# Quarter-block products in four more LSTM steps, with a new place for sums of weights and a later load of two groups of x

## The chip, the cores and the metric

The kernel runs on one core of one Trainium2 chip. The metric is the device time of one execution in microseconds; the median of three runs before the change is 2421.2 (2419.95 to 2422.31). Lower is better. All arithmetic is fp32.

## The reference

Four layers of a graph network act on x of shape 128 x 64 x 256 (128 graphs, 64 nodes, 256 features), each as `x = x + layer(max(layernorm(x), 0))`. The change lies in the first layer, in its last LSTM. That layer mixes the nodes twice with the adjacency matrix and small weights, and then runs four LSTMs, p = 1 to 4, each over windows of p consecutive nodes; the last hidden state of a window replaces its last node:

```python
def step(carry, x_t):
    h, c = carry
    g = x_t @ Wih.T + h @ Whh.T + bias
    i, f, gg, o = jnp.split(g, 4, axis=-1)
    c = jax.nn.sigmoid(f) * c + jax.nn.sigmoid(i) * jnp.tanh(gg)
    h = jax.nn.sigmoid(o) * jnp.tanh(c)
    return ((h, c), None)
...
for p in range(1, MAX_SKIP + 1):
    nw = Tv // p
    wins = h[:, :nw * p, :].reshape(Bv * nw, p, Hd)
    last = _lstm_last(Wih[p - 1], Whh[p - 1], bih[p - 1], bhh[p - 1], wins)
    idx = jnp.arange(nw) * p + (p - 1)
    h = h.at[:, idx, :].set(last.reshape(Bv, nw, Hd))
return h
```

The second layer is masked attention over the 64 nodes, the third two linear layers with batch normalization, the fourth three graph convolutions.

## The kernel before

**Tiling.** The 8192 tokens lie in 16 groups of 512 (`NG`), a group being 4 tiles of 128 tokens. Four groups (`NK` = 4) have x tiles of their own from the start, `xs[0]` to `xs[3]`, under the tags x0 to x3. The state of the first layer lies transposed in four tiles `hs[0]` to `hs[3]`, 32 graphs each, with features on the partitions.

**The LSTMs.** The loop at L896 runs p = 1 to 4. A unit (L905) is a run of windows in two of the four `hs` tiles: 256 windows of each, for p = 4. There are four units at p = 4, taken in pairs: j = 0 is the pair on `hs[0]` and `hs[1]`, j = 2 the pair on `hs[2]` and `hs[3]`. A pair first takes its first time step (`first_steps`, L762), which has no hidden state yet, and then, for t = 1 to p - 1, each unit of the pair in turn takes `next_step` (L813). So j = 2 at p = 4 has six such steps, numbered by `slot` from 0 to 5: two units at t = 1, two at t = 2, two at t = 3.

**Seven products.** A step works out two gate sets (`gate_set`, L694: i with g, then f with o). The product of a gate set's weights with x and h is a 2 x 2 block product, done with seven block products instead of eight (`seven`, L241, with the sums and differences of Winograd's form of Strassen's method). Each block product is itself a product of 2 x 2 quarter blocks of 128 x 128 weights with 256 columns of data, four matmuls of 256 columns. The profile shows an fp32 matmul as two records. The sums of weights are made once per p (`blocks_of`, L865), the differences of data by DVE in each step (L821 to L827).

**Quarter blocks.** Where a step gets `within`, two of its seven block products per gate set, numbers 6 and 2, are split once more (`Split`, L178): seven matmuls of 128 columns instead of four of 256. This needs four sums of quarter weights per split product, made once per p by `split_sums` (L885), and eight differences of quarter data per step, made by DVE in `split_differences` (L225). Each split product comes out of TensorE in two parts: `first` (four products, L197), which ACT copies out once (L207), DVE adds up (L209, L210) and POOL adds to three quarters (L213); and `last` (three products), which DVE adds (L223). Steps without `within` add a whole bank with one DVE instruction (L262) and let ACT apply a gate's function straight from the bank.

**Room.** While the LSTMs run, the tags x0 to x3 hold four scratch tiles `free[0]` to `free[3]` (L895). `free[0]` and `free[1]` hold the sums of quarter weights, `free[2]` and `free[3]` the scratch of the pair's two units. Steps have `within` at p = 2 and at p = 4 with j = 0. At p = 4 with j = 2, x is loaded again into those tags (L928 to L932), so that `within` is None there. The weights of the LSTMs and their sums lie in a pool of five tiles (`lw`, tag w). At p = 4 two of them hold the weights and two the sums that all steps use; p = 3 had used the other tiles for its weights and half of its sums.

**Beside the last six steps.** During j = 2 DVE turns the finished nodes of `hs[0]` and `hs[1]` round (`turn_nodes`, L387, two parts in each of slots 0 to 3), and SP writes them to memory as y. In slots 2 and 3, `x_for` (L372) loads four groups of x each into the tiles that `hs[0]` and `hs[1]` leave. `add_turned` (L400) is a DMA that POOL issues and that adds y to a group of x. The tuple `ADDED_BESIDE` (L167) says which groups are added in which slot, behind POOL's last sum of the step: groups 0 and 1 in slot 2, 2 and 3 in slot 3, 4 and 5 in slot 4, 6 and 7 in slot 5. In slot 4 group 0 is normalized for the attention. Groups 1 and 2 are normalized by `normalized` (L1080): group 1 at the start of the attention's first group, group 2 at its end.

**Order.** Each engine's instructions are put in order before the run by a planner that simulates their times and takes ready instructions in the order of the program text; `tc.issue_after(x)` puts an instruction behind x on its engine. Instructions may thus stand earlier or later than in the text. In the profile, attention's first matmul (L1118) starts at 1197.27 us.

Of the kernel before, what the change touches and what calls it, by code (L numbers as in the profile page):

```python
# [9 lines left out]
F32 = mybir.dt.float32  # L10
# [5 lines left out]
P = 128  # L16
D = 256
# [8 lines left out]
NK = PER  # L26
# [13 lines left out]
def adj_preln_kernel(ctx: ExitStack, tc: tile.TileContext, x_in, adj, vec, bg0, bg1,  # L40
# [17 lines left out]
    def load_x(x, g):  # L58
        nc.sync.dma_start(out=x, in_=x_view[:, g * GT : (g + 1) * GT, :])
# [104 lines left out]
    HN = GN // 2  # L164

    sums_on_pool = []
    ADDED_BESIDE = ((), (), (0, 1), (2, 3), (4, 5), (6, 7))  # L167

    def summed_last():
        return sums_on_pool[-1]  # L170
# [256 lines left out]
    with tc.tile_pool(name="lw", bufs=5) as lw:  # L427
# [6 lines left out]
        with tc.tile_pool(name="gw", bufs=1) as gw, tc.tile_pool(name="gcn", bufs=2) as gp, \  # L434
# [84 lines left out]
            for i, w_d in enumerate((wg0, wg1)):  # L519
                w = gw.tile([P, 2, D], F32, tag=f"wg{i}", name=f"wg{i}")  # L520
# [149 lines left out]
        with tc.tile_pool(name="back", bufs=1, reuse_waits="tile") as back_pool, \  # L670
# [194 lines left out]
            def blocks_of(p, wi, wh):  # L865


                wx, wm = (w.rearrange("p c (j m f) -> p m c j f", m=2, f=P) for w in (wi, wh))
                ss = []
                for tag, pool in (("w", lw), ("w", lw) if p == 4 else ("arena", keep)):  # L870
                    s = pool.tile([P, 2, 1024], F32, tag=tag, name="s")
                    ss += [s[:, :, i * 512 : (i + 1) * 512] for i in range(2)]
                ss = [s.rearrange("p c (j f) -> p c j f", f=P) for s in ss]

                def make(which):
                    sums(nc.vector, wx[:, 0], wm[:, 0], wx[:, 1], wm[:, 1], *ss, which=which)

                make(range(3))
                within = None
                if p != 3:  # L880
                    within = {}
                    for i, a, s in ((6, ss[1], free[0]), (2, wm[:, 0], free[1])):
                        blocks = [[a[:, c, 2 * r : 2 * r + 2] for c in range(2)] for r in range(2)]
                        s = s.rearrange("p a (i f) -> p a i f", f=P)
                        split_sums(nc.vector, blocks, s)  # L885
                        within[i] = blocks, s
                ws = [by_chunk([wx[:, m], wm[:, m]]) for m in range(2)] + [by_chunk(ss)]
                return ws, lambda: make([3]), within
# [7 lines left out]
            for p, nk in ((1, 8), (2, 8), (3, 7), (4, 8)):  # L896
                n = nk * HB
                wi, wh = w_next
                if p < 4:
                    w_next = (load_w(wih, p), load_w(whh, p))  # L900
                starts = range(0, NODES // p // nk * nk, nk)
                units = [(tiles, k0) for tiles in ((0, 1), (2, 3)) for k0 in starts]

                for j in range(0, len(units), 2):
                    two = [unit(p, *u, nk) for u in units[j : j + 2]]  # L905
                    first_steps(p, n, two, units[j : j + 2], w0)
                    if p > 1:
                        flush()
                        if j == 0:
                            ws, last_sum, within = blocks_of(p, wi, wh)  # L910
                    if j + 2 == len(units):
                        if p < 4:
                            w0 = first_blocks(
                                w_next[0], weight_tile(),
                                [copied_of[i] for i in (9, 14, 15, 15)] if p == 1 else None,
                            )
                        else:
                            w_att = weight_tile()
                            nc.sync.dma_start(
                                out=w_att[:, :, 0:768], in_=wqkv.rearrange("(c p) f -> p c f", p=P)  # L920
                            )
                            wqk = [[w_att[:, c, m * D : (m + 1) * D] for c in range(2)] for m in range(2)]
                            wv = w_att[:, :, 512:768]
                            ss = [w_att[:, c, 768:1024] for c in range(2)]
                            nc.vector.tensor_tensor(ss[0], wqk[1][0], wqk[1][1], ALU.add)
                            nc.vector.tensor_tensor(ss[1], ss[0], wqk[0][0], ALU.subtract)
                            nc.vector.tensor_tensor(wdiff, wqk[0][0], wqk[1][0], ALU.subtract)
                    if p == 4 and j == 2:  # L928
                        within = None
                        for g in range(NK):  # L930
                            xs[g] = xpool.tile([P, GT, D], F32, tag=f"x{g}", name=f"x{g}")
                            load_x(xs[g], g)  # L932
                    for t in range(1, p):
                        for i, u in enumerate(two):
                            stepped_before = stepped
                            stepped = next_step(
                                t, p, n, u, ws, last_sum if (j, t, i) == (0, 1, 0) else None,
                                (within, free[2 + i]) if within else None,
                            )

                            if p == 4 and j == 2:
                                slot = 2 * t + i - 2
                                if slot == 0:
                                    room = keep.tile([P, 2, TN, 2, 32], F32, tag="arena", name="turned")
                                for part in range(2 * slot, min(2 * slot + 2, 8)):
                                    turn_nodes(
                                        part,
                                        room[:, part % 3] if part % 3 < 2 else back_pool.tile(
                                            [P, TN, 2, 32], F32, tag="hc", name="turned"
                                        ),  # L950
                                    )()
                                for x_of_group in ADDED_BESIDE[slot]:
                                    with tc.issue_after(summed_last()):
                                        add_turned(x_of_group)
                                if slot in (2, 3):
                                    x_for(slot - 2)
                            if p == 4 and j == 2 and t == p - 1 and i == 0:

                                h = back_pool.tile([P, GT, D], F32, tag="hc", name="h")
                                with tc.issue_after(stepped_before):  # L960
                                    ln_relu(xs[0], h)
                                hTs = keep.tile([P, 2, 2, GN], F32, tag="arena", name="hT")
                                hT = features(transposed(h))
# [540 lines left out]
    for g in range(NG):  # L1504
        a = h1s[g]
# [83 lines left out]
    room = w_att[:, :, 512:1024]  # L1589
# [303 lines left out]
    within = None  # L1893
# [112 lines left out]
```

## Time and profile before

| | before |
|---|---|
| median of three runs | 2421.2 us |
| profiled execution | 2423.3 us |
| its span (first to last instruction) | 2421.5 us |
| mean granted clock of TensorE | 0.999 |
| DVE, ACT, POOL busy | 70%, 49%, 25% |
| p = 4, j = 0: its six split steps | 890.6 to 1033.2 us |
| p = 4, j = 2: first time step | 1033.2 to 1051.4 us |
| p = 4, j = 2: six steps | 1051.4 to 1197.3 us |

The three engines DVE, ACT and POOL work on what TensorE left in its eight banks of PSUM, and on what it will read next. The span is what the profile accounts for; the rest of the execution lies around it. In the profile a PE record's length is modelled and reaches into the next record, so the pace of matmuls is read from start to start.

### The profile page before, as it was taken

What the parts mean: (1) busy time and instruction counts of PE and PEld (TensorE: products, weight loads), DVE (VectorE), ACT (ScalarE), POOL (GpSimd) and SP (SyncE); (2) the same over time, 40 slices, a digit from 0 to 9 for tenths busy, and PEclk for the clock granted to TensorE, in tenths of its full rate; (3) what the DMA queues carried; (4) which work ended last, traced back from release to release, by engine and by line L of the source; (5) the groups of instructions that cost most, each with busy time, mean ns of one, the idle gap of its engine ahead of it and who ended that gap; (6) DMA issues with size and microseconds to landing.
All of it is one profiled execution on the core that took longest, in us unless ns stands there. A gap on an engine that the chain in (4) does not pass through costs nothing.

```text
span 2421.5 us, 49124 instructions
## 1 busy us (share of the span) xinstructions
PE 2398.7 (99%) x20272; PEld 2094.3 (86%) x20272; DVE 1685.4 (70%) x3425; ACT 1177.2 (49%) x2178; POOL 605.9 (25%) x549
## 2 busy tenths in 40 slices
PE   9999999999999999999999999999999999999999
PEld 7778888889999999988888867586898999999998
DVE  6768888777566687775599887586556655665664
ACT  4557755555444454453455556564333334333332
POOL 4432222222111112212224444123111311221121
PEclk9999999999999999999999999999999999999999
DMA  4200000001000000053347410010133100000000
GB/s 139 86 2 1 1 18 1 1 1 35 1 1 1 1 1 1 18 127 70 53 78 133 76 32 2 10 62 10 27 62 57 33 10 11 19 10 10 19 10 19
DMA packets 163712, 75.45 MB, mean 31 GB/s; under 512 B 104481, under 2 KB 159905, under 8 KB 163489
## 3 DMA queue, kind: packets, MB, share of 16 engines
q1 hardware_dynamic: 150096, 59.18, 9.8%
q0 software_dynamic: 12672, 12.58, 3.5%
q8 instruction: 159, 2.61, 0.4%
q14 instruction: 65, 0.52, 0.1%
q10 hardware_dynamic: 720, 0.56, 0.1%
HBM read 42.94 MB, written 20.97 MB: 26 GB/s over the span
## 4 chain that ended last, share of the span: by engine, by line
PE 92%; DVE 5%; ACT 2%; issue 1%; POOL 0%; DVEq 0%; ACTq 0%; POOLq 0%
PE ps L704 37%; PE ps L1772 13%; PE ps L1824 8%; PE ps L197 7%; PE ps L1700 4%; PE ps L146 4%; PE ps L1096 3%; PE ps L612 2%; PE ps L638 2%; PE ps L1470 2%; PE ps L1022 2%; PE ps L1055 2%; PE ps L1532 1%; PE ps L1118 1%; PE ps L1845 1%
## 5 line engine op out<-in xcount | busy, mean ns | idle before, releaser
L718 ACT ACTIVATE gates<-gates,lbias 128x512 f32<-128x512 f32 (+3 forms) x482 | 265.7, 605 | 173.7 <-DVE gates L272 121.6
L704 PE MATMUL ps<-diff,s 128*128 128x256 f32 (+1 forms) x1600 | 344.9, 369 | 0.5 <-DVE diff L826 0.5
L704 PEld LDWEIGHTS ps<-diff,s 128*128 128x128 f32 x1600 | 303.3, 190 | 27.5 <-issue 0.9
L1772 PE MATMUL ps<-arena 128*128 128x256 f32 x1408 | 318.5, 380 | 0.0
L267 POOL TENSOR_TENSOR gates<-p 128x512 f32<-128x512 f32 (+1 forms) x115 | 148.9, 1295 | 589.0 <-DVE p L263 518.4
L1772 PEld LDWEIGHTS ps<-arena 128*128 128x128 f32 x1408 | 261.4, 190 | 35.1 <-issue 2.0
L704 PE MATMUL ps<-h,w 128*128 128x256 f32 (+1 forms) x1028 | 242.5, 371 | 0.0
L704 PE MATMUL ps<-diff,w 128*128 128x256 f32 (+1 forms) x1040 | 239.7, 371 | 0.0
L704 PEld LDWEIGHTS ps<-diff,w 128*128 128x128 f32 x1040 | 194.8, 190 | 16.5
L704 PEld LDWEIGHTS ps<-h,w 128*128 128x128 f32 x1028 | 192.7, 190 | 17.7 <-issue 0.5
L267 POOL TENSOR_TENSOR arena<-arena 128x512 f32<-128x512 f32 (+1 forms) x80 | 91.7, 1147 | 461.9 <-DVE arena L263 407.8
L256 ACT COPY p<-ps 128x512 f32<-128x512 f32 (+1 forms) x262 | 142.1, 563 | 60.1 <-PE ps L704 39.7
L350 ACT ACTIVATE arena<-arena 128x512 f32<-128x512 f32 x168 | 98.5, 624 | 121.4 <-POOL arena L267 66.5
L256 ACT COPY arena<-ps 128x512 f32<-128x512 f32 (+1 forms) x160 | 82.2, 517 | 149.6 <-PE ps L1700 59.5
L1824 PE MATMUL ps<-arena 128*128 128x128 f32 x1280 | 149.1, 275 | 0.8 <-DVE arena L339 0.8
L1824 PEld LDWEIGHTS ps<-arena 128*128 128x128 f32 x1280 | 146.7, 192 | 2.1 <-DVE arena L339 1.2
L718 ACT ACTIVATE gates<-ps,lbias 128x256 f32<-128x256 f32 (+2 forms) x157 | 68.2, 479 | 143.9 <-PE ps L704 143.8
L339 DVE TENSOR_TENSOR arena<-arena 128x512 f32<-128x512 f32 (+1 forms) x192 | 111.3, 612 | 29.4 <-ACT arena L350 27.8
L207 ACT COPY free<-ps 128x128 f32<-128x128 f32 x104 | 27.6, 265 | 208.0 <-PE ps L197 208.0
L272 DVE TENSOR_TENSOR gates<-p,ps 128x512 f32<-128x512 f32 (+1 forms) x115 | 76.3, 664 | 65.0 <-PE ps L704 64.2
L704 PE MATMUL ps<-state,s 128*128 128x256 f32 (+1 forms) x512 | 116.3, 370 | 0.6 <-ACT p L256 0.6
L272 DVE TENSOR_TENSOR arena<-arena,ps 128x512 f32<-128x512 f32 (+1 forms) x80 | 48.1, 601 | 87.0 <-PE ps L1824 50.4
(270 smaller groups left out, 4831.0 us busy)
## 6 DMA issues: line engine op xcount, KB each, us to landing
x<-in_x SPq DMA_DIRECT2D x23, 512.0 KB, 4.0
y<-turned SPq DMA_DIRECT2D x64, 128.0 KB, 3.3
v<-vt SPq DMA_DIRECT2D x128, 64.0 KB, 2.6
w<-in_wih SPq DMA_DIRECT2D x4, 1024.0 KB, 7.2
x_for_h<-in_x SPq DMA_DIRECT2D x8, 512.0 KB, 6.9
x<-y POOLq DMA_DIRECT2D x8, 512.0 KB, 6.3
x_for_h<-y POOLq DMA_DIRECT2D x8, 512.0 KB, 6.7
z<-w SPq DMA_DIRECT2D x64, 64.0 KB, 2.0
```

The costliest lines, as they stand in the source:

```text
L146: last = nc.tensor.matmul(pss[b][half * 64 : half * 64 + 64, c, t, :], lhsT=src[rows, t, col : col + 64], rhs=a2[rows, :], start=True, sto ...
L197: nc.tensor.matmul(q[k], lhsT=w, rhs=b, start=first and k == 0, stop=True, skip_group_check=True)
L256: copied = nc.scalar.copy(p1 if i == 1 else p5, ps[i])
L267: nc.gpsimd.tensor_tensor(out=out[1][1], in0=p1, in1=p5, op=ALU.add).ins
L272: nc.vector.tensor_tensor(out[0][1], p1, ps[5], ALU.add)
L339: last = eng.tensor_tensor(out=s, in0=p, in1=q, op=op)
L350: nc.scalar.activation(o, o, func)
L704: nc.tensor.matmul(ps[:, r], lhsT=wc[:, j, :], rhs=bc, start=first and r == 0 and c == 0, stop=True, skip_group_check=True,)
L718: nc.scalar.activation(o, ps, func, bias=lbias[:, col : col + 1])
L1700: nc.tensor.matmul(ps[:, t, :], lhsT=w[:, t * P : (t + 1) * P], rhs=b, start=first and t == 0, stop=True, skip_group_check=True,)
L1772: nc.tensor.matmul(ps[:, r, :], lhsT=w[:, c, col : col + P], rhs=b[:, c, :], start=first and r == 0 and c == 0, stop=c == 1, skip_group_ch ...
L1824: nc.tensor.matmul(ps[:, t, :], lhsT=w[:, c, t * P : (t + 1) * P], rhs=b[:, c, :], start=first and t == 0 and c == 0, stop=c == 3, skip_gr ...
```

## The change

At p = 4, the sums of quarter weights go into a weights tile of the pool `lw` (two halves of a new tile), no longer into `free[0]` and `free[1]`. At the start of j = 2 only groups 0 and 1 of x are loaded, into the tags x0 and x1. `within` is kept through t = 1 and t = 2, that is, slots 0 to 3; the scratch tiles `free[2]` and `free[3]` stay in use until then. Before t = 3, `within` becomes None and groups 2 and 3 of x are loaded into x2 and x3. Their y is added in slot 5, ahead of that of groups 6 and 7, which makes four additions in slot 5 and none in slot 3.

```diff
-    ADDED_BESIDE = ((), (), (0, 1), (2, 3), (4, 5), (6, 7))
+    ADDED_BESIDE = ((), (), (0, 1), (), (4, 5), (2, 3, 6, 7))
...
                 within = None
                 if p != 3:
                     within = {}
-                    for i, a, s in ((6, ss[1], free[0]), (2, wm[:, 0], free[1])):
+                    room = free[:2]
+                    if p == 4:
+                        w = lw.tile([P, 2, 1024], F32, tag="w", name="s")
+                        room = [w[:, i].rearrange("p (a d) -> p a d", d=D) for i in range(2)]
+                    for i, a, s in ((6, ss[1], room[0]), (2, wm[:, 0], room[1])):
                         blocks = [[a[:, c, 2 * r : 2 * r + 2] for c in range(2)] for r in range(2)]
                         s = s.rearrange("p a (i f) -> p a i f", f=P)
                         split_sums(nc.vector, blocks, s)
...
-                    if p == 4 and j == 2:
-                        within = None
-                        for g in range(NK):
+                    def x_again(gs):
+                        for g in gs:
                             xs[g] = xpool.tile([P, GT, D], F32, tag=f"x{g}", name=f"x{g}")
                             load_x(xs[g], g)
+
+                    if p == 4 and j == 2:
+                        x_again(range(2))
                     for t in range(1, p):
+                        if p == 4 and j == 2 and t == p - 1:
+                            within = None
+                            x_again(range(2, NK))
                         for i, u in enumerate(two):
```

## The prediction

> **What bounds the kernel now.** I read the page's head and its busy row first, then a table of stretches around the six last LSTM steps, then TensorE's own order of instructions in a step that already has quarter-block products and in one that has none.
>
> ```profile
> span 2421.5 us, 49124 instructions
> ...
> PE 2398.7 (99%) x20272; PEld 2094.3 (86%) x20272; DVE 1685.4 (70%) x3425; ACT 1177.2 (49%) x2178; POOL 605.9 (25%) x549
> ```
>
> TensorE is busy for 99% of the span, so time comes from fewer or shorter matmuls, as long as no other engine makes it wait. The next question is whether it waits in these steps. Columns: stretch, its length, then busy time and count for PE, weight loads, DVE, ACT and POOL, clock, DMA share and GB/s.
>
> ```profile
> 890.62:914.39 23.77, 23.77 (x138) 21.53 (x137) 21.10 (x50) 11.23 (x24) 7.24 (x6) 1.00 0.00 1
> 926.44:950.25 23.81, 23.81 (x138) 21.45 (x137) 17.73 (x39) 11.27 (x23) 6.85 (x7) 1.00 0.01 2
> ...
> 1053.09:1077.26 24.17, 24.17 (x114) 21.22 (x112) 16.65 (x26) 10.47 (x21) 3.44 (x2) 1.00 0.81 165
> 1077.26:1101.43 24.17, 24.17 (x113) 21.28 (x112) 16.05 (x20) 9.33 (x18) 2.83 (x2) 1.00 0.56 121
> 1101.43:1125.60 24.17, 24.17 (x113) 21.28 (x112) 13.58 (x16) 9.32 (x18) 5.59 (x4) 1.00 0.22 53
> ```
>
> The trace of before holds both kinds of step. The first two rows are the first and a middle step of p = 4, j = 0, which have quarter-block products; the last three are the first steps of j = 2, which have none. One step takes 23.81 us with them and 24.17 without, at a granted clock of 1.00 in both. PE is full in every row. Where the next row's DVE stands matters too: 17.7 of 23.8 in the middle split step, 16.65 and 16.05 already in the first two unsplit ones, because there DVE also turns finished nodes round.
>
> **The change, part by part.** The saving first. TensorE in the first half of a split step, then in an unsplit one (start, length, line, what, how many):
>
> ```profile
> 931.62 0.38 PE L197 MATMUL ps<-diff,s 128*128 128x128 f32 x2
> 931.84 0.39 PE L197 MATMUL ps<-free,free 128*128 128x128 f32 x2
> ...
> 935.80 1.89 PE L704 MATMUL ps<-diff,w 128*128 128x256 f32 x8
> 937.53 0.38 PE L197 MATMUL ps<-state,w 128*128 128x128 f32 x2
> ```
>
> ```profile
> 1106.61 1.89 PE L704 MATMUL ps<-state,w 128*128 128x256 f32 x8
> 1108.34 1.89 PE L704 MATMUL ps<-state,s 128*128 128x256 f32 x8
> ```
>
> Eight records of 256 columns take 1.73 us from start to start (1108.34 - 1106.61), 0.216 each; two of 128 columns take 0.22 (931.84 - 931.62), 0.111 each. A product that is split becomes fourteen records of 128 in place of eight of 256: 14 x 0.111 = 1.56 against 1.73, 0.17 us saved. Two products per gate set, two gate sets per step, four steps: 16 x 0.17 = 2.7 us at best. The measured split step gives less: 24.17 - 23.81 = 0.36 instead of 0.68, because its second gate set (938.20 to 950.25) takes 12.05 against 11.76 for its first; the order there has gaps of about 0.1 us between a product of one kind and the next. I take the measured step: 4 x 0.36 = **1.4 us**, with 2.7 kept as the upper end of the gain.
>
> The Trainium skill, "TensorE: Matmul & The Clock Gate", section "Back-to-back issue gap", speaks against the change: it says that in a stream of weight load and matmul pairs the load sets the pace at small widths, about 81 ns at 128 columns against 131 at 512. My estimate from those two figures, on a straight line, is 98 ns at 256, and by it 14 x 81 - 8 x 98 is a loss of 0.35 us per product, 5.6 us over sixteen. The rows above have 128 columns at almost exactly half of 256, so here the load stays hidden and the sum goes by the rows.
>
> DVE next. Against an unsplit step without transposes (13.58), a middle split step has 17.73, so the edit adds about 4.2 us of DVE per step: eight differences of 0.29 us (they start 0.20 apart), four corrected sums, less two sums that go. That makes 20.9, 20.3, 17.8 and 17.8 of 23.8 in the four steps. No step is over its time, and the first split step of j = 0 shows 21.10 busy with PE full and only one wait of weight loads for a difference (0.17 us). So I cost DVE at 0 beyond what the measured split step holds. The cover is thin in the first two: 2.9 and 3.5 us. If it is gone, the first correction product is late. Ahead of it DVE could have at worst two transposes (0.63 each), three sums of attention weights (0.34 each) and one 1.22 us product, 3.5 us in each of two steps; TensorE has 3.5 us of other products before it needs the differences. Bounds: 0 to 3.5 us twice, and I take 0, since the nearest row, the first split step, lost 0.17.
>
> ACT gains about 1.9 us per step (9.33 to 11.27) and POOL about 4 (2.83 to 6.85), both far from full. POOL's work has a second price: a DVE difference that runs beside POOL's last sum took 1.76 us where its usual length is 0.69, and the change adds four POOL sums of 1.0 us per step. The measured split step carries the same four, so this is inside the 0.36.
>
> The sums of weights (two sets of four, eight DVE operations of 0.41, 3.3 us at 869 to 872) now go to a weights tile instead of two x tiles. At p = 4 the five weights tiles have four live (two of weights, two of sums), so one is free, but it was last read by p = 3. DVE's first two sums into reused tiles start at 863.62 and 867.43, as p = 3's last products release them; the third tile is free at the latest when p = 3's last product ends at 872.5. The eight sums may thus stand 0 to 3.5 us later. Their first reader starts at 895.8, and DVE has 3.5 us idle between 880 and 890. I take 0. Behind them on DVE would stand two sums that empty banks at 872.5; those banks are wanted two gate sets of first_steps later, some 6 us, so even 3.5 us costs nothing there.
>
> The loads. x0 and x1 no longer wait for the last j = 0 step: their tiles are idle from p = 2 on. x2 and x3 move behind the second pair of steps, on the queue of SP behind the eight loads of x_for, and wait there for the last reader of their tiles, the steps that end near 1125 and 1149. SP's next work is at 1203, so nothing stands behind them. A load of x lands in 3.7 to 8.3 us, so by about 1157.
>
> ```profile
> 1169.30 2.62 POOL L404 DMA_DIRECT2D x_for_h<-y  x2
> 1181.05 1.26 POOL L267 TENSOR_TENSOR gates<-p 128x512 f32<-128x512 f32 x1 [9.13 <-DVE p L263]
> 1193.20 1.27 POOL L267 TENSOR_TENSOR gates<-p 128x512 f32<-128x512 f32 x1 [10.89 <-DVE p L263]
> 1194.41 2.60 POOL L404 DMA_DIRECT2D x_for_h<-y  x2
> 1205.59 1.27 POOL L267 TENSOR_TENSOR k<-p 128x512 f32<-128x512 f32 x1 [8.58 <-DVE p L263]
> ```
>
> Their two additions move from the fourth step to the sixth, which then issues four: 4 x 1.3 = 5.2 us on POOL from 1194.4, to 1199.6; the next POOL instruction starts at 1205.6, so 6.0 us of cover remain. The fourth step's POOL loses the 2.6 us it now gains elsewhere. x2, the first in line, lands 5.7 to 9.5 us after issue, at 1204 at the latest; the first instruction that reads it is a statistic on DVE at 1215.0, so 11 us of cover. Two such transfers kept the DMA engines moving for 7 us (1123 to 1130), so four would end near 1210, and x3, x6 and x7 are read after x2. If the cover went, DVE would stand at that statistic, with the first attention group's transposes and sums queued behind it. I cost it at 0; bounds 0 to 3.
>
> **Sum.** -1.4 us. The profiled execution took 2423.3 (span 2421.5, 1.8 around it) and would take 2421.9; it stands 2.1 above the median of the three runs, 2421.2, which becomes **2419.8**. Below about 4.8 us (0.2%) a measurement of this kernel can't tell a change from none, so this is "the same". Its own range is 2418.5 (all of the 2.7) to 2421.5 (small waits eat it).
>
> **Rivals.** First, **DVE decides the first two steps**. For it: 16.65 and 16.05 us of work there already, and a transpose may be written ahead of a difference on its queue. Against it: the first split step of j = 0 had as much DVE work and lost next to nothing. It decides once DVE is more than 3.5 us behind at the first correction product. Price: 3.5 us twice less 1.4 saved, 2421.2 + 7.0 - 1.4 = 2426.8.
>
> Second, **the written order shifts elsewhere**. A planner that simulates times writes each engine's order; with changed instructions it may order attention's entry differently, where TensorE waits 0.7 us in 24 (23.31 busy from 1197 to 1221). Both signs: some eight groups by 0.4 us, 3 us, give 2416.8 or 2422.8; more than that needs a much worse order.
>
> Third, **the late x**: x2's addition is held behind its load or three others. It decides once x2 lands after 1215; ending 3 us late costs 2421.2 - 1.4 + 3 = 2422.8. Against it: 11 us of cover.
>
> Fourth, the change **does less than it says**: only 0.1 us per step survives because the same gaps come in both gate sets; 2420.8.
>
> **Chances.** Forecast 0.52, does less 0.14, DVE 0.16, order 0.14 (half on each side), late x 0.04. Of the DVE case 0.10 lies above 2426.0, and of the late x and the order another 0.05; the order's good side passes 2416.4 with 0.05. So faster 0.05, same 0.80, slower 0.15. The range leaves 0.07 below 2416.8 and 0.12 above 2425.5: 2416.8 to 2425.5.
>
> **What would show it.** Right: four steps of j = 2 at 23.8 us each and the last two at 24.2, PE without waits between them, about 1.4 us less to the first matmul of attention, four additions in a row on POOL before 1200 and the first statistic of x2 without a wait. Wrong: a weight load that waits for a difference on DVE in the first or second step (DVE), a step of 11.76 twice over (the full 2.7), a wait of DVE for a DMA at x2 (late x), or TensorE's idle time after 1195 changed by over 1 us (order). Forecast and rivals all fall if a step gets longer without a wait.

## The result and the profile after

The changed kernel takes 2428.25 us, the median of nine runs (2425.49 to 2431.81), against 2422.36 for nine runs of the kernel before on the same chip (2419.95 to 2423.74). The ratio is 1.0027, with a 95% interval of 1.0016 to 1.0037: **5.9 us slower**, where 1.4 us of gain were forecast, and 2.75 us above the range. The page of the changed kernel, head, busy row and the queue that brings instructions:

```profile
span 2426.4 us, 49473 instructions
...
PE 2396.8 (99%) x20368; PEld 2094.6 (86%) x20368; DVE 1701.8 (70%) x3513; ACT 1184.0 (49%) x2202; POOL 621.2 (26%) x565
...
q8 instruction: 160, 2.62, 0.5%
```

The span is 4.9 us longer, but TensorE's modelled busy time is 1.9 us less: it does less work and stands idle more. The start times of the same landmarks in the two traces say where (us, a stretch runs from one landmark to the next):

```
stretch                                               before    after   change
start to the first quarter product of p = 4           895.80   895.41    -0.39
... to attention's first matmul (L1118 / L1127)       301.47   302.74    +1.27
... to the third layer's first (L1022 / L1031)        224.55   229.23    +4.68
... to its products in seven (L1055 / L1064)           31.46    29.48    -1.98
... to the last layer's products (L1772 / L1781)      224.78   224.77    -0.01
... to the last matmul                                739.04   740.33    +1.29
```

So the edited steps cost 1.3 us in place of gaining 1.4, and most of the loss lies in the attention, whose arithmetic and data are untouched, and whose 2992 matmul records stand in the same order in both traces. (The -1.98 is mostly three matmul records of 512 columns at 1443 to 1447 that took 0.85 to 1.0 us each, not 0.43, in this one execution of the kernel before, and 0.4 less of a wait for ACT. It belongs to single executions: e3 and e6 below, with the instruction count of the kernel before, take 29.88 and 29.89 there, e1 and e5 29.88, and e9 31.46 again.)

**The edited steps.** The table of stretches of the changed kernel answers to the one of before: first split step of j = 0, then slots 0 to 3 of j = 2 (stretch, length, busy time and count of PE, weight loads, DVE, ACT, POOL, clock, DMA share, GB/s):

```profile
890.23:914.92 24.69, 23.96 (x136) 21.22 (x136) 21.33 (x50) 12.45 (x26) 7.30 (x6) 1.00 0.00 1
1053.51:1078.36 24.85, 24.15 (x137) 21.41 (x136) 23.23 (x57) 11.17 (x23) 6.64 (x6) 1.00 0.54 94
1078.36:1102.35 23.99, 23.89 (x137) 21.37 (x136) 18.97 (x41) 11.68 (x25) 6.85 (x6) 1.00 0.65 148
1102.35:1126.16 23.81, 23.81 (x137) 21.45 (x136) 18.16 (x37) 11.19 (x23) 8.70 (x8) 1.00 0.25 75
1126.16:1150.65 24.49, 24.00 (x138) 21.45 (x137) 17.17 (x32) 11.15 (x24) 7.67 (x7) 1.00 0.35 66
```

Slot 2 is the forecast's 23.81 exactly. The other three have lost 1.04, 0.18 and 0.68 against it, and in each PE is busy for less than the stretch. The four take 97.14, against 4 x 24.17 = 96.68 before and 95.24 forecast. And j = 0's first split step, which the change does not split anew, has grown from 23.77 to 24.69.

**The attention.** TensorE's timeline of the changed kernel around 1250 us (start, length, what, how many, and in brackets the idle time before it and its releaser):

```profile
1250.88 1.16 PE L1201 MATMUL ps<-v,eT 64*64 64x64 f32 x64
1251.87 1.09 PE L1152 MATMUL ps<-k,q 64*64 64x64 f32 x58
1254.26 0.34 PE L1152 MATMUL ps<-k,q 64*64 64x64 f32 x6 [1.30 <-issue]
...
1314.41 2.64 PE L1127 MATMUL ps<-w,hT 128*128 128x256 f32 x6 [1.26 <-issue]
...
1426.53 0.92 PE L1152 MATMUL ps<-k,q 64*64 64x64 f32 x44 [1.11 <-issue]
```

The same run of matmuls in the kernel before:

```profile
1250.02 1.16 PE L1192 MATMUL ps<-v,eT 64*64 64x64 f32 x64
1251.00 1.11 PE L1143 MATMUL ps<-k,q 64*64 64x64 f32 x64
1252.05 1.99 PE L1118 MATMUL ps<-w,hT 128*128 128x256 f32 x8
```

The same 128 records, without a hole. In the changed kernel the hole falls after the 58th score product. No engine and no DMA of data is named as releaser, only "issue": the instruction itself was late.

What the holes share is their place in TensorE's stream of instructions. Queue 8 brought 2.62 MB in 160 transfers, 16 KB each; TensorE's trace has 41,106 instructions (each record is a weight load and a matmul, and there are semaphore instructions), so one transfer carries about 257, as near to 256 as the count can tell. The waits for issue after 1195 us are 4 before the change (3.7 us in all) and 10 after it (9.6):

```profile
PE ps L146 <- issue: 4.2, 5, 1.1
PE ps L1152 <- issue: 3.5, 3, 1.3
...
PE ps L1127 <- issue: 1.3, 1, 1.3
```

Each line gives the total, the count and the longest (the tenth, 0.6 us, is at L1781). Counted through the two traces, all fourteen end at index 192 or 193 of a period of 256 (some instructions leave no record, so only the period means something, not the 192). Some of them, with the gap from one weight load's start to the next:

```
                 wait ends at   index mod 256   gap between starts   fetch that ended before it
before, L146        1915.23         193              1.13            1912.62 to 1913.97
before, L146        1963.08         193              1.36            1960.38 to 1961.48
after,  L1152       1254.26         192              1.57            1251.37 to 1252.85
after,  L1152       1283.19         192              1.36            1280.62 to 1281.69
after,  L1127       1314.40         192              1.85            1312.11 to 1313.05
after,  L1152       1426.53         192              1.38            1424.13 to 1425.03
after,  L146        1872.76         192              1.34            1869.89 to 1871.29
```

A block's border has a fixed place in the stream. In these fourteen places the fetch of the next block takes 0.9 to 1.5 us, and that block's first instruction starts 2.3 to 2.9 us after the fetch began. The fetch began 0.7 to 1.2 us after TensorE entered the current block, 2.5 in one place. So the wait ends 3.1 to 3.6 us after the entry in twelve places, and 4.1 and 4.8 in the other two. (At the 4.1, TensorE enters a block at 1250.18, the next one is fetched from 1251.37 to 1252.85, and its first instruction starts at 1254.26.) Matmuls of 256 columns take far longer over 256 instructions than that (128 records of 0.216 us are 28 us), but the attention's 64 x 64 products put 256 instructions (128 records) into the 2.0 us between 1250.02 and 1252.05. If a block's whole length falls into such a run, TensorE waits at its end, unless the fetch began earlier. In the kernel before, the block from 1865.37 to 1867.23 passes in 1.9 us without a wait, the next one's fetch having begun at 1864.39, ahead of the entry. The change added 96 records, that is 192 instructions, and 17 semaphore instructions, and so moved every border after p = 4 by 209 instructions. The four waits before are all in the last layer; of the ten after, four are in the attention.

### The profile page after: what moved, and what is told of

The parts are those of the page before. It is cut to its first block, busy times and chain, and to the rows that moved or that the text cites. A ratio compares the mean times of both kernels' runs of the same rounds, so it can differ in the third digit from the quotient of the medians.

```text
span 2426.4 us, 49473 instructions
## 1 busy us (share of the span) xinstructions
PE 2396.8 (99%) x20368; PEld 2094.6 (86%) x20368; DVE 1701.8 (70%) x3513; ACT 1184.0 (49%) x2202; POOL 621.2 (26%) x565
## 3 DMA queue, kind: packets, MB, share of 16 engines
q8 instruction: 160, 2.62, 0.5%
## 4 chain that ended last, share of the span: by engine, by line
PE 91%; DVE 5%; ACT 2%; issue 1%; POOL 0%; DMA 0%; SPq 0%; DVEq 0%; ACTq 0%; POOLq 0%
PE ps L704 35%; PE ps L1781 13%; PE ps L1833 8%; PE ps L197 8%; PE ps L1709 4%; PE ps L146 4%; PE ps L1105 3%; PE ps L612 2%; PE ps L638 2%; PE ps L1479 2%; PE ps L1031 2%; PE ps L1064 2%; PE ps L1127 2%; PE ps L1541 1%; PE ps L1854 1%
## 5 line engine op out<-in xcount | busy, mean ns | idle before, releaser
L718 ACT ACTIVATE gates<-gates,lbias 128x256 f32<-128x256 f32 (+3 forms) x498 | 272.2, 602 | 172.8 <-DVE gates L272 118.7
L704 PE MATMUL ps<-diff,s 128*128 128x256 f32 (+1 forms) x1536 | 331.3, 369 | 0.7 <-DVE diff L826 0.5
L1781 PE MATMUL ps<-arena 128*128 128x256 f32 x1408 | 318.5, 380 | 0.6 <-issue 0.6
L704 PEld LDWEIGHTS ps<-diff,s 128*128 128x128 f32 x1536 | 291.2, 190 | 26.1 <-issue 1.4
L1781 PEld LDWEIGHTS ps<-arena 128*128 128x128 f32 x1408 | 261.5, 190 | 35.7 <-issue 2.5
L267 POOL TENSOR_TENSOR gates<-p 128x512 f32<-128x512 f32 (+1 forms) x115 | 147.8, 1285 | 516.5 <-DVE p L263 439.7
L267 POOL TENSOR_TENSOR arena<-arena 128x512 f32<-128x512 f32 (+1 forms) x80 | 91.7, 1146 | 461.7 <-DVE arena L263 423.4
L718 ACT ACTIVATE gates<-ps,lbias 128x256 f32<-128x256 f32 (+2 forms) x141 | 61.4, 479 | 113.2 <-PE ps L704 113.0
L272 DVE TENSOR_TENSOR gates<-p,ps 128x512 f32<-128x512 f32 (+1 forms) x115 | 76.1, 662 | 54.0 <-PE ps L704 53.0
L213 POOL TENSOR_TENSOR p<-p,free 128x384 f32<-128x384 f32 x36 | 36.3, 1008 | 285.1 <-DVE free L210 251.6
```

The source lines that it names most:

```text
L267: nc.gpsimd.tensor_tensor(out=out[1][1], in0=p1, in1=p5, op=ALU.add).ins
L272: nc.vector.tensor_tensor(out[0][1], p1, ps[5], ALU.add)
L704: nc.tensor.matmul(ps[:, r], lhsT=wc[:, j, :], rhs=bc, start=first and r == 0 and c == 0, stop=True, skip_group_check=True,)
L718: nc.scalar.activation(o, ps, func, bias=lbias[:, col : col + 1])
L1781: nc.tensor.matmul(ps[:, r, :], lhsT=w[:, c, col : col + P], rhs=b[:, c, :], start=first and r == 0 and c == 0, stop=c == 1, skip_group_ch ...
```

## The experiments

Theory A (borders) says that the 4.7 us are the place of the instruction blocks and follow the instruction count alone; its rival, theory B, says that the change disturbs attention through data, order or DVE. For the other 1.3 us the theories are: S, the sums of quarter weights come too late; D, DVE is late in slots 0 and 1; P, the additions on POOL stand in front of POOL's sum in slot 2. The kernel before was run beside each group: its medians are 2422.18 (27 runs) for e1 to e4, 2422.54 (27) for e5 to e8, 2422.45 (26) for e9 to e11.

### e1_pad12: the changed kernel, with borders put back

Twelve more 64 x 64 matmuls stand in slot 4 and write into a bank that is then overwritten. Each is two records, four instructions: 209 + 48 = 257, one block and one instruction more than before.

```diff
-    def transposed(src):
-        pss = [bank() for _ in range(2)]
+    def transposed(src, filler=0):
+        pss, one = [bank() for _ in range(2)], ident[0:64, 0:64]
+        for _ in range(filler): nc.tensor.matmul(pss[0][0:64, 0:64], lhsT=one, rhs=one, start=True, stop=True)
...
-                                hT = features(transposed(h))
+                                hT = features(transposed(h, 12))
```

> The changed kernel with 12 tiny 64x64 matmuls (48 TensorE instructions, about 0.4 us) ahead of the transposes that open attention; their result is overwritten. Everything else is in the same order. Theory A (instruction blocks): the change's 209 extra TensorE instructions moved the borders of the 256-instruction blocks into dense runs of small matmuls; 48 more bring them to within 1 of where they lay before the change. The waits for issue of over 0.8 us after 1195 us fall from 10 to 4 and the time falls by 3 to 5 us, to 2423.5 to 2425.5. Theory B (the planner's order or the four additions made attention slower): no change or +0.4, 2428 to 2429.

Measured: 2425.25 us (2423.41 to 2428.25, 11 runs), ratio 1.0013 (1.0004 to 1.0022). That is 3.0 below the changed kernel, although the filler lengthens its gate set from 12.96 to 14.65 us. The attention takes 224.28, as before the change (224.55), without one wait for issue; after 1195 us five of them are left, 3.2 us in all. More work made it faster: 3.0 + 1.7 = 4.7 us came from moving borders, and the attention alone is 4.95 shorter. Theory B has no place for that.

### e2_pad52_before: the kernel before, with the changed kernel's borders

This is the same edit on the kernel before, `features(transposed(h, 52))`. It has 208 instructions more, the changed kernel's count but for one.

> The kernel before the change with 52 tiny 64x64 matmuls (208 TensorE instructions, 104 records of about 17 ns, 1.8 us) ahead of the transposes that open attention; their result is overwritten. Nothing of the change is in it. Theory A (instruction blocks): borders now lie where the changed kernel has them, so about 10 waits for issue of over 0.8 us instead of 4, and the time is 1.8 + 3 to 5 us over before: 2427 to 2429. Theory B (order, additions): +1.8 only, 2424.2.

Measured: 2434.88 us (2432.41 to 2436.17, 5 runs), ratio 1.0052 (1.0039 to 1.0065), 12.7 over the kernel before. TensorE's timeline has the filler:

```profile
1171.69 6.28 PE L125 MATMUL ps<-ident 64*64 64x64 f32 x104
```

It cost 6.4 us (its gate set went from 12.96 to 19.32), not the 1.8 I had reckoned: the attention's 0.017 us per record holds where the kernel sends products to the four quarters of the array in turn, and with all of them in one quarter a record takes 0.061. What is left, 6.3 us, lies in the attention above all: 229.99 us to the third layer's first product, 5.4 more than before, with TensorE's waits there as in the changed kernel:

```profile
PE ps L1143 <- issue: 4.8, 4, 1.7
PE ps L146 <- issue: 3.3, 5, 1.0
...
PE ps L1118 <- issue: 1.3, 1, 1.3
```

None of the change is in this kernel, and the attention loses as much and a little more. Theory A stands from both sides.

### e5_pad17: borders 20 instructions further

This is e1 with 17 matmuls in place of 12.

> As e1_pad12 with 17 tiny matmuls in place of 12, so the borders lie 20 instructions further on; nothing else differs, and the five more matmuls themselves cost 0.6 us (0.12 each, as measured in e1 and e2). Theory A (instruction blocks): from the start times of e1's instructions, the borders then miss attention's dense runs, but in the last layer more than the four blocks of e1 pass in under 3.4 us: no wait for issue of over 0.8 us in attention, more than four of them after 1800 us, and 2 to 5 us over e1. Theory B (blocks are no cause, e1 gained by chance): e1 + 0.6.

Measured: 2429.87 us (2427.88 to 2432.54, 5 runs), ratio 1.0033 (1.0021 to 1.0046), 4.6 over e1 (4.3, each against the kernel before beside it) for a filler that costs 0.6 more. The attention has no wait for issue. TensorE's waits after 1195 us, in the kernel before, e1 and e5 (in total, how many, the longest):

```profile
PE ps L146 <- issue: 3.7, 4, 1.2
```

```profile
PE ps L146 <- issue: 2.8, 4, 0.9
```

```profile
PE ps L146 <- issue: 6.0, 7, 1.2
```

At these times L146 is the last layer's run of 64 x 64 products. Now these lose: 3.2 us more than in e1, of the 3.7 to 4.0 to be explained. So the instruction count is a dial that sets several microseconds. It decides the attention in all thirteen traces: 224.3 to 224.6 us with 40,897, 41,153, 41,154 or 41,174 TensorE instructions, and 229.2 and 230.0 with 41,106 and 41,105. An estimate, from stepping a border through the start times of e4's trace with 3.4 us per block, finds 6 us lost in all at the place of before, 12.7 at that of the changed kernel and up to 15 at others: by it the kernel before sits near the cheapest place. It counts too much, since the waits in the traces sum to 3.7 and 9.6 us and it leaves out fetches that begin early; its differences are what it is good for.

### e3_moves_only and e6_sums_free: without the new splits

In e3 the four steps of j = 2 keep whole products; the sums' new tile and the late x2 and x3 stay. In e6 the sums go back to `free[0]` and `free[1]` as well, so only the late x is left.

```diff
                     if p == 4 and j == 2:
+                        within = None
                         x_again(range(2))
```

```diff
-                    if p == 4:
+                    if p == 5:
                         w = lw.tile([P, 2, 1024], F32, tag="w", name="s")
```

> The changed kernel without the four added quarter-block steps: only the sums of weights in the weights tile, the late load of x2 and x3 and their late addition. Theory: the moves cost 0.4 us at the first split step of p = 4 (its differences stand behind the moved sums on DVE) and nothing else, so 2422.4 + 0.4, within 1 us of before, with the block borders within a few instructions of before. Rival (the four additions in a row or the late x2 cost attention): 2424 or more, with waits at the first statistic of x2.

> As e3_moves_only, with the sums of quarter weights back in free[0] and free[1]; only the late load and addition of x2 and x3 is left of the change. Theory: the first split step of p = 4 loses 0.9 us in the changed kernel and in e3 because the sums wait for a weights tile that p = 3 still reads; here it is as before (the first product of quarter blocks is followed by product 3 after 1.14 us, not 2.00), and the kernel is within 0.5 us of before. Rival (the loss comes from x0 and x1 being loaded earlier): 2.00 stays.

Measured: e3 2422.22 us (2421.43 to 2426.84, 11 runs), ratio 1.0004 (0.9995 to 1.0013); e6 2422.24 (2420.36 to 2424.70, 11 runs), 0.9997 (0.9988 to 1.0005). Neither time can be told from no change, but the stretches can. From the first quarter product to attention's first matmul: before 301.47, e3 302.33, e6 301.46. So the late x costs nothing, and the sums' new place costs 0.86 (0.4 was expected), all of it at the first split step of j = 0. There TensorE's timeline in the kernel before, then in the changed one, reads:

```profile
895.80 0.38 PE L197 MATMUL ps<-diff,s 128*128 128x128 f32 x2
...
896.94 1.89 PE L704 MATMUL ps<-state,s 128*128 128x256 f32 x8
```

```profile
895.41 0.38 PE L197 MATMUL ps<-diff,s 128*128 128x128 f32 x2
896.25 0.49 PE L197 MATMUL ps<-free,s 128*128 128x128 f32 x2 [0.46 <-DVE free L231]
896.86 0.49 PE L197 MATMUL ps<-diff,s 128*128 128x128 f32 x2
897.19 0.39 PE L197 MATMUL ps<-free,s 128*128 128x128 f32 x2
897.41 1.89 PE L704 MATMUL ps<-state,s 128*128 128x256 f32 x8
```

From 895.41 to 897.41 is 2.00; before it is 895.80 to 896.94, 1.14. TensorE waits for a difference of data, and not for a sum of weights. DVE's timeline, before and then after, shows why:

```profile
872.18 0.41 DVE L339 TENSOR_TENSOR free<-s,free 128x256 f32<-128x256 f32 x1
...
884.40 1.22 DVE L798 TENSOR_TENSOR state<-gates 128x1024 f32<-128x1024 f32 x1 [1.52 <-ACT gates L718]
```

```profile
881.01 1.48 DVE L339 TENSOR_TENSOR s<-w 128x256 f32<-128x256 f32 x1
882.41 0.41 DVE L339 TENSOR_TENSOR s<-w,s 128x256 f32<-128x256 f32 x1
882.75 0.67 DVE L272 TENSOR_TENSOR gates<-p,ps 128x512 f32<-128x512 f32 x1
...
886.14 1.23 DVE L798 TENSOR_TENSOR state<-gates 128x1024 f32<-128x1024 f32 x1 [1.52 <-ACT gates L718]
...
893.98 0.28 DVE L231 TENSOR_TENSOR free<-state 128x128 f32<-128x128 f32 x1
```

The last four sums now stand at 879.7 to 882.8; before, all eight were over at 872.6. Behind them stands the sum of gates that ACT needs (L272, 881.33 before), behind ACT's sigmoid the first state (L798, 884.40 before), and behind that the differences. Against the first product of the split step (892.35 before, 891.57 after) L798 comes 2.5 us later, and the differences still 1.3.

### e10_adds_order: the sums into a tile that is free earlier

This is e4 (below) with the tiles handed out in another order, so that the quarter sums take the second tile that comes free, and the third set of whole sums the last.

```diff
                 for tag, pool in (("w", lw), ("w", lw) if p == 4 else ("arena", keep)):
+                    if p == 4 and ss: w = lw.tile([P, 2, 1024], F32, tag="w", name="s")
                     s = pool.tile([P, 2, 1024], F32, tag=tag, name="s")
...
-                make(range(3))
+                make(range(2 if p == 4 else 3))
...
-                        w = lw.tile([P, 2, 1024], F32, tag="w", name="s")
+                        pass
...
+                if p == 4: make([2])
```

> As e4_pad12_adds, with the quarter-weight sums of p = 4 taking the weights tile that is free second, so that DVE makes them before the last two whole sums as it did before the change, and those whole sums wait for the third tile instead. Theory (the 0.9 us at the first split step of p = 4 is DVE work pushed behind p = 3's last product): product 3 follows the first quarter product after 1.2 to 1.6 us, not 2.00, and 0.4 to 0.9 us under e4. Rival (any third tile costs the same, since two more DVE sums of 1.2 us are now late): 2.0 stays.

Measured: 2423.42 us (2422.30 to 2426.09, 11 runs), ratio 1.0006 (0.9996 to 1.0015). TensorE's timeline:

```profile
897.27 0.38 PE L198 MATMUL ps<-diff,s 128*128 128x128 f32 x2
...
898.40 1.89 PE L705 MATMUL ps<-state,s 128*128 128x256 f32 x8
```

From the first quarter product to product 3 it is 1.13 again, a little under the 1.2 to 1.6 expected, and e4's 303.99 to the attention becomes 303.13: the 0.86 are back. S is shown by adding it (e3) and by taking it away (e6, e10).

### e4_pad12_adds: the additions behind POOL's last sum

This is e1 with slot 2's two additions issued behind POOL's last three-quarter sum (L213).

```diff
-            nc.gpsimd.tensor_tensor(out=three, ...)
+            threes_added.append(nc.gpsimd.tensor_tensor(out=three, ...).ins)
...
-                                    with tc.issue_after(summed_last()):
+                                    with tc.issue_after(threes_added[-1] if within else summed_last()):
```

> As e1_pad12, and POOL issues the additions of groups 0 and 1 behind the third-step pair's last POOL sum of three quarters instead of ahead of it. Theory: in the changed kernel the two additions stood ahead of that sum and made DVE late, which cost the fourth step (slot 3) 0.6 us: it takes 24.5 us there, and 23.8 here; 0.6 us under e1. Rival (slot 3 is slow because DVE is full): no change in slot 3.

Measured: 2423.68 us (2422.47 to 2429.03, 11 runs), ratio 1.0010 (1.0002 to 1.0019); below e1, but the intervals overlap. The time from slot 3's first gate set to its second goes from 12.73 to 12.23 us, 0.5 of the 0.6 expected. POOL's timeline in the changed kernel, then in e4:

```profile
1122.04 1.27 POOL L267 TENSOR_TENSOR gates<-p 128x512 f32<-128x512 f32 x1 [0.86 <-DVE p L223]
1123.26 1.47 POOL L404 DMA_DIRECT2D x<-y  x1
1124.31 1.46 POOL L213 TENSOR_TENSOR gates<-gates,free 128x384 f32<-128x384 f32 x1
1125.27 1.77 POOL L404 DMA_DIRECT2D x<-y  x1
```

```profile
1121.63 1.27 POOL L268 TENSOR_TENSOR gates<-p 128x512 f32<-128x512 f32 x1 [0.85 <-DVE p L224]
1123.14 1.00 POOL L214 TENSOR_TENSOR gates<-gates,free 128x384 f32<-128x384 f32 x1 [0.24 <-DVE free L211]
1124.08 2.80 POOL L405 DMA_DIRECT2D x<-y  x2
```

`issue_after(summed_last())` puts them behind the newest sum on POOL that `summed_last` knows, L267; in a split step a three-quarter sum, L213, follows it. One addition took its place ahead of L213, which then ran from 1124.3 to 1125.8 instead of ending at 1124.1, and DVE's difference beside it took 1.77 us instead of 0.69:

```profile
1124.57 1.77 DVE L821 TENSOR_TENSOR diff<-h,h 128x512 f32<-128x512 f32 x1
1126.26 0.54 DVE L223 TENSOR_TENSOR gates<-gates,ps 128x384 f32<-128x384 f32 x1
```

The state of that step is late after them, and in the next step TensorE waits for a sum of a part (L210). P is worth 0.50.

### e8_whole_adds and e7_warm_adds: DVE in the first two slots

e7 is e4 with the filler at the kernel's start, where TensorE is kept busy anyway (19 small matmuls in place of 7 large); e8 is e7 with slot 0 unsplit again, and 32 small matmuls to hold the borders.

```diff
-            keep_busy(7)
+            for _ in range(19): nc.tensor.matmul(idle[0:64, 0:64], lhsT=ones[0:64, 0:64], rhs=ones[0:64, 0:64], start=True, stop=True)
```

```diff
-                            (within, free[2 + i]) if within else None,
+                            (within, free[2 + i]) if within and (p, j, t, i) != (4, 2, 1, 0) else None,
```

> The changed kernel, with the additions of e4, and with the 48 instructions that bring the block borders back placed at the very start, where TensorE waits for x: 19 tiny matmuls in place of 7 of 128x128. Theory: no cost for the filler, so e4 less 1.7 us: 2421.5 to 2422.5, level with before; the four added steps save 1.4 us and lose as much to the moved sums (0.9) and to DVE in the first two (0.7).

> As e7, but the first of the four added steps (unit 0, t = 1) is left without quarter blocks, which takes their work from DVE there; filler for the same borders. Theory (DVE is too late in the first two of the steps): the gate sets that took 12.62 and 12.20 us take 12.09 and 11.76 to 12.05, at most 0.5 us better than e7 although one split step, 0.36 us, is given up. Rival (the lateness comes from the second unit's own work): they stay above 12.2.

Measured: e7 2423.90 us (2422.67 to 2427.24, 11 runs), ratio 1.0010 (1.0001 to 1.0019); e8 2427.26 (2425.94 to 2429.39, 11 runs), 1.0021 (1.0012 to 1.0029). Both totals miss, since the filler was not free at the start. TensorE's timeline, e7 and then e8:

```profile
1.04 4.32 PE L466 MATMUL ps<-ones 64*64 64x64 f32 x38 [1.04 <-DVE ones L447]
```

```profile
1.05 7.08 PE L466 MATMUL ps<-ones 64*64 64x64 f32 x64 [1.05 <-DVE ones L447]
```

0.11 us per record there, where slot 4's took 0.06, so the first product of the program starts at 8.20 and 10.98 instead of 7.44. The rows of the steps are clean, though. Time from one gate set to the next, each taken at its product 3 (us; "to 0" leads from j = 0's last gate set to slot 0's first, "in 0" from slot 0's first to its second, and so on; "to 0" and "to 4" also hold that product 3 stands earlier in a split set):

```
           to 0   in 0   to 1   in 1   to 2   in 2   to 3   in 3   to 4   in 4   to 5
before    32.45  12.09  12.09  12.09  12.09  12.09  12.09  12.09  12.09  12.09  12.96
after     30.36  11.76  12.62  12.20  11.80  12.05  11.76  12.73  14.32  12.09  12.96
e7        30.36  11.76  12.63  12.21  11.80  12.05  11.76  12.23  14.32  12.09  12.96
e8        32.45  12.09   9.52  12.13  11.76  12.05  11.76  12.23  14.32  12.09  12.96
```

In j = 0 the steady split sets alternate between 11.76 and 12.05 ("to" and "in"), so after loses 0.86, 0.15 and 0.04 in a row from "to 1" on, and 0.68 at "in 3". From "to 0" to "to 4", before takes 129.17 us, after 129.60, e7 129.12 and e8 128.31. e8 has one split step fewer than e7 and is 0.8 us shorter: D holds, and it is the first of the four steps that brings the lateness. The changed kernel's TensorE shows the wait there:

```profile
1070.09 1.89 PE L704 MATMUL ps<-state,s 128*128 128x256 f32 x8
1072.56 0.68 PE L197 MATMUL ps<-diff,s 128*128 128x128 f32 x4 [0.58 <-DVE free L210]
```

DVE waits 0.96 us for POOL's three-quarter sum until 1066.52, and has no idle time from there to that L210, at 1072.14: nine differences, a product of gates and three sums stand in a row before it. The nine are not slot 0's own but slot 1's. In slot 0's stretch of the changed kernel DVE makes sixteen quarter differences (L231), eight for each unit of the pair, in those of slots 1 and 2 eight, and in that of slot 3 none.

### e9_adds_wqk and e11_adds_both: DVE's other work moved off

e9 is e4 with the three sums of attention weights (L929 to L931) moved behind slot 3 in the text; e11 adds the order of e10, with 32 x 32 filler to make it cheaper.

> As e4_pad12_adds, with DVE's three sums of attention weights (1.0 us) moved from the first of the four added steps to the fifth step. Theory (DVE's own backlog makes the first two added steps late): the gate sets of 12.62 and 12.20 us shorten by 0.3 to 0.7 in all; the rest as e4, so up to 0.7 us under it. Rival (the lateness is in ACT or POOL): unchanged.

> e9 and e10 together, with the 12 tiny matmuls 32x32 in place of 64x64, which should cost less than their 1.7 us. Theory: all three sources of the lost gain mended (additions, backlog, sums) and borders back; p = 4 takes 1.0 to 1.4 us less than before the change, plus the filler; 2421.5 to 2422.5, at best 0.5 us under before, too little to tell.

Measured: e9 2424.11 us (2422.89 to 2426.70, 11 runs), ratio 1.0005 (0.9996 to 1.0015); e11 2422.99 (2420.74 to 2425.26, 11 runs), 1.0003 (0.9994 to 1.0012). In e9 the planner, which may place text early, moved the sums by only 12 us, from 1059 to 1071.5 to 1073.8, still in slot 0's stretch; so they were not taken off the two late steps as intended. The two late gate sets became 12.53 and 12.06, 0.24 shorter, where 0.3 to 0.7 was expected. e11 has everything that was found. Its stretch from the first quarter product to the attention is 302.20 us with a filler of 1.02 in it, 301.18 without, 0.3 less than before the change, where 1.0 to 1.4 was expected. It is level with the kernel before and 5 us better than the changed one; no version here beats the kernel before by what a measurement can tell.

## Why the prediction was wrong, point by point

- **Saving: mechanism right, size right where nothing waits.** Slot 2 takes 23.81, its gate sets 12.05 and 11.76, as the forecast took them from j = 0; a record of 128 columns kept its 0.111 us, and no loss by weight loads showed there.
- **The instructions themselves: the step that failed most, 4.7 us.** The sum priced 96 more records as matmuls and gave nothing for the code that they are. The rival "the written order shifts elsewhere" named the attention's entry as the place, but its mechanism was a new order; the order is the same, and what moved is where blocks of 256 instructions end. With before's borders (e1) these 4.7 us are gone, and with the changed kernel's borders the attention of the kernel before loses 5.4 (e2). The cue was in the profile of before: queue 8 with 159 transfers of 16 KB, and four waits for issue of 0.6 to 1.2 us in the last layer.
- **The sums of weights, "I take 0": 0.86.** The delay was seen (0 to 3.5 us), but cover was counted to the sums' own reader at 895.8. What mattered was behind the sums on DVE: a gate sum, then ACT, then a state, then the differences. The 3.5 us of idle DVE were waits, 1.52 for ACT (L798) and the rest for TensorE, and no room for work that delays what ACT waits for.
- **DVE in the first two steps, "I take 0 ... the nearest row, the first split step, lost 0.17": 1.05.** That is 0.86 + 0.15 + 0.04 from slot 0's second gate set on. DVE was busy for 23.2 us in slot 0, not 20.9. The sum gave every step eight quarter differences, and the stretch of slot 0 has sixteen. The eight more, 0.20 us apart, make 1.6 of the missing 2.3, and a fourth transpose, where before had three, 0.6. The rival named the right place and the right wait, at a seventh of its price of 7.0; e8 shows that it is slot 0's split that brings it. The row I took as nearest, the first split step of j = 0, has sixteen too, but no transposes (slot 0 has four) and no sums of attention weights (three).
- **POOL's additions, inside "the 0.36" too: 0.50 of slot 3's 0.68.** j = 0's steps carry the same POOL sums, but no additions between them (e4). The other 0.18 stays open.
- **Late x2 and x3, costed at 0: right.** POOL's timeline at the end of slot 5 in the changed kernel:

```profile
1195.27 2.59 POOL L404 DMA_DIRECT2D x<-y  x2
1196.81 3.66 POOL L404 DMA_DIRECT2D x_for_h<-y  x2
1206.45 1.27 POOL L267 TENSOR_TENSOR k<-p 128x512 f32<-128x512 f32 x1 [5.98 <-DVE p L263]
```

Four additions end at 1200.5 (1199.6 forecast), the next POOL work comes 6 us later, and e6, which has only this move, keeps the stretches of the LSTM and the attention (301.46 and 224.34). The first statistic of x2 starts at 1215.84, without a wait.

Together, for p = 4: -1.44 + 0.86 + 1.05 + 0.68, and 0.14 because the way into and out of the split sets ("to 0" and "to 4", 44.68 against 44.54) is no gain, make +1.29; the landmarks have +1.27. With the attention's 4.68 this is 5.95, against 5.9 between the medians. The 2.0 given back at the entry to the third layer belong to single executions, as e3, e6 and e9 show. The last layer's 1.3 stays open: its waits for issue are 1.1 more than before (4.8 against 3.7), but e2, with borders one instruction away, has 3.3 there and takes 739.01.

One slip lies in the chances: the prediction gives 0.15 to a time above 2426.0, yet only 0.12 to one above 2425.5.

## What to carry to other kernels

Instructions have a place as well as a price: where TensorE runs many small matmuls, adding some anywhere earlier cost or gained about 4 to 6 us here, so a small change in time is only a verdict on an edit once it is measured at equal instruction counts modulo the block (a filler of known cost does it). When an operation is moved on a full engine, count the cover of what stands behind it on that engine and of what the next engine makes of that, not only of its own reader. And look in the row of the very stretch for idle time: an engine that waits for a neighbour has no room for work that the neighbour waits for.

## What the runs showed of the hardware that was not expected

- TensorE's instructions come in blocks of 256, 16 KB each. Where it waited, the next block's fetch took 0.9 to 1.5 us and its first instruction started 2.3 to 2.9 us after the fetch began, 3.1 to 4.8 after the block before was entered. The waits before and after were up to 1.3 us, and 1.7 in e2. The Trainium skill, "Runtime: NRT & Kernel Launch", section "Instruction fetch mechanics", has the same blocks of 16 KiB and 256 instructions, and says that crossing a border is mostly hidden. That agrees with the LSTMs here, whose runs of 256 columns show no wait for issue in either profile; in runs of 64 x 64 products it doesn't hold, and there the measurement decides.
- 64 x 64 fp32 records cost 0.017 us when sent to four quarters of the array in turn (64 in 1.1 us), 0.06 to 0.07 when all go to one quarter (e1, e2), and 0.11 at the very start of the program (e7, e8). e11's 32 x 32 records took 0.04.
- A DVE difference of 512 columns that started beside a sum on POOL ended 0.55 us after that sum: it took 1.77 us in the changed kernel (L821 at 1124.57, the sum until 1125.78), its usual length being 0.69. The kernel before has the same with 1.76 us (L826 at 1083.92, the sum until 1085.13), and there POOL issued no transfer meanwhile.
